# Attention stage: row sums taken on GpSimd and VectorE, reciprocals transposed on TensorE, and one timetable for a group of pixels

## The chip, the core and the metric

The kernel runs on one core of one Trainium2 chip. The metric is the device time of one execution in microseconds (us). A core has four compute engines that run side by side, each through its own instructions in order, and that wait for each other by semaphores: TensorE (PE in the profile, with its weight loads as PEld), VectorE (DVE), ScalarE (ACT) and GpSimd (POOL). SyncE (SP) issues the transfers. SBUF is the working memory; PSUM takes TensorE's results, and this kernel uses it in banks of 512 float32 columns.

## What is computed

The input x has 128 images of 128 channels and 32 x 32 pixels. Two layers follow each other; only the first, an attention layer, is touched by the change. Each of the 1024 pixels is a sequence of its own: the 128 images at that pixel attend to each other, with 4 heads of 32 channels.

```python
xs = x.reshape(B, C, L).transpose(2, 0, 1)                 # L=1024 pixels, B=128, C=128
q, k, v = jnp.split(xs @ in_proj_weight.T + in_proj_bias, 3, axis=-1)
q = q * float(hd) ** (-0.5)                                # 4 heads, hd = 32
scores = jnp.einsum('lhbd,lhed->lhbe', q, k)               # 128 x 128 per pixel and head
attn = jax.nn.softmax(scores, axis=-1)
out = jnp.einsum('lhbe,lhed->lhbd', attn, v)
y = out @ out_proj_weight.T + out_proj_bias + xs
y = (y - mu) * jax.lax.rsqrt(var + LN_EPS) * norm_weight + norm_bias
```

The second layer (convolutions and a selective scan, one image after the other) reads the first layer's result from the DRAM tensor `mid`.

## The kernel before

`attention_layer` works on groups of LG = 4 pixels, 256 groups in all. Channels lie on the partitions. SyncE brings 64 pixels of all images at a time into `xt` (two buffers), and results leave from `yt` (two buffers). All data are float32.

A group goes through these steps:

- GpSimd gathers its columns into `xg` (L221).
- TensorE projects q and k (L168, 512 columns each) and v (L233, per pixel). VectorE moves q out of PSUM with bias and scale (L209), ScalarE moves k (L226), VectorE moves v (L240).
- Scores (L142): per pixel and head one product of 32 rows, into the four PSUM banks of `s_ps`, one bank per head. A pixel's four heads use the four 32-row strips of the array at the same time.
- Softmax in two halves of two pixels: VectorE takes the maximum of each row (`top`, L152), VectorE subtracts it (`shifted`, L156) into `e`, ScalarE takes the exponential (`exps`, L165).
- Per pixel, TensorE transposes the four heads of `e` (L178); the result is copied to `eT`, by ScalarE for three pixels (L254, L256, L267) and by VectorE for one (L258).
- `weighted` (L183) multiplies twice per pixel: `eT` with v (the weighted sum, not yet divided) and `eT` with a matrix of ones 32 columns wide, so that each row sum comes out of TensorE and stands at once on all 32 channels of its head. Both use 32-column strips of the array, four heads at the same time.
- ScalarE forms the reciprocal of the sums as exp(-ln(sum)) into `rden` (L201, L202) and VectorE multiplies (L203, `oT`).
- Output projection with the mean over channels already taken off, and the residual, add up in one bank (L217, L218); ScalarE squares (L219), TensorE averages over channels (L228), ScalarE forms 1/sqrt as exp(-0.5 ln) (L229, L230), VectorE applies it (L242, `z`), GpSimd applies weight and bias into `yt` (L243).

The order on every engine is written out by hand in `tick`: one call issues the scores of one group, the transposes of the group before it, the end of the one before that, and so on, so that a period of all engines is one tick. Four PSUM banks (`m_ps`) are handed round in a fixed pattern. The constants of the second layer (`mamba_constants`, a generator) are prepared in pieces between the first ticks. Its first piece issues some thirty small weight loads on SyncE; here it stands behind the load of the first `xt`.

The second layer already uses another scheme: class `Plan` collects tasks with a name, an engine, the buffers that they read and write and the banks that they take and give. Each name has a due time in a table, tasks of image i are due i periods later, and `run` issues everything in order of due time. A due time only sets the order on each engine; nothing waits for a clock. `Plan` reads its table and period from the module's `AT` and `PERIOD`.

Of the kernel before, what the change touches and what calls it, by code (L numbers as in the profile page):

```python
# [50 lines left out]
@with_exitstack  # L51
def attention_layer(ctx: ExitStack, tc: tile.TileContext, ident, eps, x, w, mid, prepare):

    nc = tc.nc
    const = ctx.enter_context(tc.tile_pool(name="a_const", bufs=1))
    keep = ctx.enter_context(tc.tile_pool(name="a_keep", bufs=1))

    qkvT = const.tile([P, 3 * P], F32, name="qkvT")  # L60
    nc.sync.dma_start(qkvT, w["qkvT"])
    outT = const.tile([P, P], F32, name="outT")
    nc.sync.dma_start(outT, w["outT"])
    bqkv = const.tile([P, 3], F32, name="bqkv")
    nc.sync.dma_start(bqkv, w["qkv_b"])
    bo = const.tile([P, 1], F32, name="bo")
    nc.sync.dma_start(bo, column(w["out_b"]))
    nw = const.tile([P, 1], F32, name="nw")
    nc.sync.dma_start(nw, column(w["norm_w"]))
    nb = const.tile([P, 1], F32, name="nb")  # L70
    nc.sync.dma_start(nb, column(w["norm_b"]))
    qscale = float(HD) ** -0.5

    mean = const.tile([P, P], F32, name="a_mean")
    nc.vector.memset(mean, 1.0 / P)
    ones = const.tile([P, HD], F32, name="ones")
    nc.vector.memset(ones, 1.0)
    om = const.tile([P, 1], F32, name="om")  # L80
    nc.vector.reduce_sum(om, outT, AX.X)
    nc.vector.tensor_scalar_mul(om, om, 1.0 / P)
    outc = const.tile([P, P], F32, name="outc")
    nc.vector.tensor_scalar(outc, outT, om, None, ALU.subtract)
    resc = const.tile([P, P], F32, name="resc")
    nc.vector.tensor_sub(resc, ident, mean)
    by = const.tile([P, 1], F32, name="by")
    with tc.tile_pool(name="a_prep_ps", bufs=1, space=PSUM) as prep_ps:
        b_ps = prep_ps.tile([P, 1], F32, name="by_ps")
        nc.tensor.matmul(b_ps, lhsT=outc, rhs=bqkv[:, 2:3], start=True, stop=False)  # L90
        nc.tensor.matmul(b_ps, lhsT=resc, rhs=bo, start=False, stop=True)
        nc.vector.tensor_copy(by, b_ps)

    psum = ctx.enter_context(tc.tile_pool(name="a_psum", bufs=1, space=PSUM))
    xcol = x.rearrange("b c l -> c b l")
    ycol = mid.rearrange("b c l -> c b l")

    def several(n, shape, name, pool=keep):
        return [pool.tile(shape, F32, name=f"{name}{j}") for j in range(n)]

    GB = LG * NB
    PER = LB // LG
    xts = several(2, [P, NB, LB], "xt")
    xgs = several(4, [P, GB], "xg")
    yts = several(2, [P, NB, LB], "yt")
    qTs = several(2, [P, GB], "qT")
    kTs = several(2, [P, GB], "kT")
    vs = several(4, [P, LG, P], "v")
    es = several(2, [P, NH, LG, NB], "e")
    eTs = several(LG, [P, NH * NB], "eT")  # L110
    oT = keep.tile([P, GB], F32, name="oT")
    z = keep.tile([P, GB], F32, name="z")
    tops = several(2, [P, NH, LG // 2], "top")
    sq = keep.tile([P, GB], F32, name="sq")
    rden = keep.tile([P, GB], F32, name="rden")
    s_ps = psum.tile([P, NH, LG, NB], F32, name="s_ps")
    m_ps = several(4, [P, GB], "m_ps", psum)

    def load(l0, xt):
        for s in range(4):  # L120
            bs = slice(s * NB // 4, (s + 1) * NB // 4)
            nc.sync.dma_start(xt[:, bs, :], xcol[:, bs, ds(l0, LB)])

    def store(l0, yt):
        for s in range(4):
            bs = slice(s * NB // 4, (s + 1) * NB // 4)
            nc.sync.dma_start(ycol[:, bs, ds(l0, LB)], yt[:, bs, :])

    def pixels(ts, g):

        i = g % PER
        return ts[g // PER % 2][:, :, i * LG : (i + 1) * LG].rearrange("c b l -> c l b")

    def heads(h):
        return slice(h * HD, (h + 1) * HD)

    def scores(g, half):

        for i in range(half * LG // 2, (half + 1) * LG // 2):
            cs = slice(i * NB, (i + 1) * NB)  # L140
            for h in range(NH):
                nc.tensor.matmul(  # L142
                    s_ps[:, h, i, :],
                    lhsT=qTs[g % 2][heads(h), cs],
                    rhs=kTs[g % 2][heads(h), cs],
                    start=True,
                    stop=True,
                )

    def top(half):  # L150
        ls = slice(half * LG // 2, (half + 1) * LG // 2)
        nc.vector.tensor_reduce(tops[half], s_ps[:, :, ls, :], AX.X, ALU.max)  # L152

    def shifted(g, half):
        ls = slice(half * LG // 2, (half + 1) * LG // 2)
        nc.vector.tensor_tensor(  # L156
            es[g % 2][:, :, ls, :],
            s_ps[:, :, ls, :],
            tops[half].unsqueeze(3).to_broadcast([P, NH, LG // 2, NB]),
            ALU.subtract,  # L160
        )

    def exps(g, half):
        ls = slice(half * LG // 2, (half + 1) * LG // 2)
        nc.scalar.activation(es[g % 2][:, :, ls, :], es[g % 2][:, :, ls, :], AF.Exp)  # L165

    def project(g, j, bank):
        nc.tensor.matmul(  # L168
            bank,
            lhsT=qkvT[:, j * P : (j + 1) * P],  # L170
            rhs=xgs[g % 4],
            start=True,
            stop=True,
        )

    def transposed(g, i, bank):
        for h in range(NH):
            nc.tensor.transpose(bank[:, h * NB : (h + 1) * NB], es[g % 2][:, h, i, :], ident)  # L178

    def weighted(g, i, lhsT, bank):  # L180

        for h in range(NH):
            nc.tensor.matmul(  # L183
                bank[heads(h), i * NB : (i + 1) * NB],
                lhsT=lhsT(h),
                rhs=eTs[i][:, h * NB : (h + 1) * NB],
                start=True,
                stop=True,
            )

    def tick(t, p, a, s, c, d, y):

        pv, den, free, other = m_ps if t % 2 else (m_ps[3], *m_ps[1:3], m_ps[0])

        if s is not None:
            scores(s, 0)
            scores(s, 1)
        if d is not None:  # L200
            nc.scalar.activation(rden, den, AF.Ln)  # L201
            nc.scalar.activation(rden, rden, AF.Exp, scale=-1.0)  # L202
            nc.vector.tensor_mul(oT, pv, rden)  # L203
        if c is not None:
            exps(c, 0)
            exps(c, 1)
        if a is not None:
            project(a, 0, free)
            nc.vector.tensor_scalar(  # L209
                qTs[a % 2], free, bqkv[:, 0:1], qscale, ALU.add, ALU.mult  # L210
            )
        if s is not None:
            top(0)
            shifted(s, 0)
            top(1)
        if y is not None:
            nc.tensor.matmul(other, lhsT=resc, rhs=xgs[y % 4], start=True, stop=False)  # L217
            nc.tensor.matmul(other, lhsT=outc, rhs=oT, start=False, stop=True)  # L218
            nc.scalar.activation(sq, other, AF.Square, bias=by)  # L219
        if p is not None:  # L220
            nc.gpsimd.tensor_copy(  # L221
                xgs[p % 4].rearrange("c (l b) -> c l b", l=LG), pixels(xts, p)
            )
        if a is not None:
            project(a, 1, den)
            nc.scalar.activation(kTs[a % 2], den, AF.Identity, bias=bqkv[:, 1:2])  # L226
        if y is not None:
            nc.tensor.matmul(pv, lhsT=mean, rhs=sq, start=True, stop=True)  # L228
            nc.scalar.activation(sq, pv, AF.Ln, bias=eps)  # L229
            nc.scalar.activation(sq, sq, AF.Exp, scale=-0.5)  # L230
        if a is not None:
            for i in range(LG):
                nc.tensor.matmul(  # L233
                    free[:, i * P : (i + 1) * P],
                    lhsT=xgs[a % 4][:, i * NB : (i + 1) * NB],
                    rhs=qkvT[:, 2 * P : 3 * P],
                    start=True,
                    stop=True,
                )
            nc.vector.tensor_copy(vs[a % 4].rearrange("p l d -> p (l d)"), free)  # L240
        if y is not None:
            nc.vector.scalar_tensor_tensor(z, other, by, sq, ALU.add, ALU.mult)  # L242
            nc.gpsimd.tensor_scalar(  # L243
                pixels(yts, y),
# [1244 lines left out]
```

## Time and profile before

| What | us |
|---|---|
| Time, median of 3 runs | 15043.29 |
| lowest and highest of them | 15040.22 and 15054.52 |
| Profiled execution | 15073.08 |
| its span, first to last instruction | 15071.3 |
| first and last result of the attention stage (L243) | 60.93 and 2846.71 from the span's start |
| one tick of the attention stage (L243 at 1498.90 and at 1509.79) | 10.89 |

| Engine | busy us | share of the span |
|---|---|---|
| PE | 13455.7 | 89% |
| DVE | 13733.7 | 91% |
| ACT | 12058.3 | 80% |
| POOL | 12317.6 | 82% |

The span runs from the first instruction to the last; the small rest of the profiled execution lies around it. A profile line names the line of the kernel, the engine, the operation, output <- inputs, the shapes, a count and times. A float32 product is recorded as two passes, a transpose as one, so a 512-column product counts x2.

### The profile page before, as it was taken

What the parts mean: (1) busy time and instruction counts of PE and PEld (TensorE: products, weight loads), DVE (VectorE), ACT (ScalarE), POOL (GpSimd) and SP (SyncE); (2) the same over time, 40 slices, a digit from 0 to 9 for tenths busy, and PEclk for the clock granted to TensorE, in tenths of its full rate; (3) what the DMA queues carried; (4) which work ended last, traced back from release to release, by engine and by line L of the source; (5) the groups of instructions that cost most, each with busy time, mean ns of one, the idle gap of its engine ahead of it and who ended that gap; (6) DMA issues with size and microseconds to landing.
All of it is one profiled execution on the core that took longest, in us unless ns stands there. A gap on an engine that the chain in (4) does not pass through costs nothing. (4 is left out here: it accounts for less than half of the span.)

```text
span 15071.3 us, 229111 instructions
## 1 busy us (share of the span) xinstructions
PE 13455.7 (89%) x87094; PEld 6624.5 (44%) x87094; DVE 13733.7 (91%) x8754; ACT 12058.3 (80%) x19718; POOL 12317.6 (82%) x4361
## 2 busy tenths in 40 slices
PE   9999999888888888888888888888888888888887
PEld 6666666433333333333333333333333333333333
DVE  6777777599999999999999999999999999999999
ACT  5666666688888888888888888888888888888887
POOL 1222222299999999999999999999999999999999
PEclk9999999899999999999999999999999999999999
DMA  3222222266676666666666666666666666666665
GB/s 57 50 57 46 46 46 46 67 169 169 169 169 169 168 169 169 168 168 169 169 168 168 168 168 169 168 169 168 169 167 169 168 168 169 169 169 169 167 168 146
DMA packets 1191603, 2180.96 MB, mean 145 GB/s; under 512 B 673233, under 2 KB 674273, under 8 KB 1190497
## 3 DMA queue, kind: packets, MB, share of 16 engines
q1 hardware_dynamic: 1190496, 2166.31, 59.6%
q8 instruction: 682, 11.17, 0.3%
q14 instruction: 425, 3.47, 0.1%
HBM read 1746.30 MB, written 419.43 MB: 144 GB/s over the span
## 5 line engine op out<-in xcount | busy, mean ns | idle before, releaser
L1216 POOL TENSOR_TENSOR dbu<-dtxr,brep 128x2048 f32<-128x2048 f32 x1280 | 5805.4, 4552 | 27.7 <-DMA dtr<-dtd 13.3
L1262 POOL TENSOR_TENSOR hc<-hc,crep 128x1024 f32<-128x1024 f32 x2304 | 5412.3, 2372 | 310.5 <-PE da L1209 211.1
L1241 ACT ACTIVATE da<-dtr,aneg 128x1024 f32<-128x1024 f32 x2560 | 2956.6, 1163 | 510.3 <-DVE hc L1262 489.3
L1254 DVE TENSOR_TENSOR_SCAN hc<-da,dbu 128x1024 f32<-128x1024 f32 x1408 | 3162.1, 2276 | 103.6 <-ACT da L1241 94.9
L1155 ACT ACTIVATE bx<-p_ps,bT 128x128 f32<-128x128 f32 (+1 forms) x8192 | 2798.0, 486 | 132.1 <-PE p_ps L1147 131.9
L1254 DVE TENSOR_TENSOR_SCAN da<-da,dbu 128x1024 f32<-128x1024 f32 x1152 | 2622.7, 2287 | 115.3 <-ACT da L1241 106.9
L1209 PE MATMUL da<-ident,bx 128*128 128x128 f32 x12288 | 1828.7, 295 | 501.1 <-DVE hc L1254 417.6
L1209 PEld LDWEIGHTS da<-ident,bx 128*128 128x128 f32 x12288 | 1489.7, 150 | 1634.3 <-DVE hc L1254 1068.5
L1262 DVE TENSOR_TENSOR hc<-da,crep 128x1024 f32<-128x1024 f32 x1792 | 2162.8, 1219 | 47.8 <-PE y_ps L1281 6.5
L769 PE MATMUL p_ps<-tn,wk 128*128 128x512 f32 x4096 | 1989.5, 608 | 240.4 <-DVE tn L733 147.2
L1241 ACT ACTIVATE dbu<-dtr,aneg 128x1024 f32<-128x1024 f32 x1536 | 1734.3, 1218 | 473.2 <-DMA dtr<-dtd 471.1
L1254 DVE TENSOR_TENSOR_SCAN hc<-dbu,da 128x1024 f32<-128x1024 f32 x896 | 2000.1, 2268 | 24.3 <-ACT dbu L1241 21.4
L1281 PE MATMUL y_ps<-hc,fold 128*32 128x512 f32 x16384 | 1974.3, 599 | 37.6 <-POOL hc L1262 25.8
L1254 DVE TENSOR_TENSOR_SCAN da<-dbu,da 128x1024 f32<-128x1024 f32 x640 | 1451.1, 2282 | 196.4 <-PE da L1209 132.6
L221 POOL COPY xg<-xt 128x512 f32<-128x512 f32 x256 | 270.4, 1057 | 1223.2 <-PE m_ps L217 1199.3
L830 PE MATMUL p_ps<-xpad,dwd 64*64 64x512 f32 x9216 | 1153.4, 593 | 112.8 <-ACT xm L801 105.3
L769 PEld LDWEIGHTS p_ps<-tn,wk 128*128 128x128 f32 x4096 | 710.6, 191 | 1141.6 <-issue 776.3
L243 POOL TENSOR_SCALAR yt<-z,nw,nb 128x512 f32<-128x512 f32 x256 | 320.2, 1251 | 1032.7 <-DVE z L242 1032.7
L1281 PEld LDWEIGHTS y_ps<-hc,fold 128*32 128x32 f32 x16384 | 477.0, 109 | 1182.9 <-issue 858.3
L830 PEld LDWEIGHTS p_ps<-xpad,dwd 64*64 64x64 f32 x9216 | 362.4, 133 | 802.4 <-issue 568.4
L1025 POOL TENSOR_TENSOR dtt<-dtt,xm 128x1024 f32<-128x1024 f32 x256 | 608.5, 2377 | 120.9 <-DMA dtd<-dtt 109.8
L203 DVE TENSOR_TENSOR oT<-m_ps,rden 128x512 f32<-128x512 f32 x256 | 177.0, 691 | 566.2 <-ACT rden L202 566.2
(131 smaller groups left out, 19281.3 us busy)
## 6 DMA issues: line engine op xcount, KB each, us to landing
dtxr<-dtxd SPq DMA_DIRECT2D x2048, 256.0 KB, 5.5
dtr<-dtd SPq DMA_DIRECT2D x2048, 256.0 KB, 5.4
crep<-bcd SPq DMA_DIRECT2D x2048, 128.0 KB, 6.2
brep<-bcd SPq DMA_DIRECT2D x1536, 128.0 KB, 5.0
x<-mid SPq DMA_DIRECT2D x256, 512.0 KB, 5.9
dtd<-dtt SPq DMA_DIRECT2D x256, 512.0 KB, 5.2
dtxd<-dtt SPq DMA_DIRECT2D x256, 512.0 KB, 4.4
xt<-in_x SPq DMA_DIRECT2D x64, 1024.0 KB, 12.2
```

The source lines that it names most:

```text
L221: nc.gpsimd.tensor_copy(xgs[p % 4].rearrange("c (l b) -> c l b", l=LG), pixels(xts, p))
L243: nc.gpsimd.tensor_scalar(pixels(yts, y), z.rearrange("c (l b) -> c l b", l=LG), nw, nb, ALU.mult, ALU.add,)
L769: nc.tensor.matmul(a.tile, lhsT=wk[:, k, h * P : (h + 1) * P], rhs=tn[:, c * CH + k : (c + 1) * CH + k], start=k == 0, stop=c > 0 and k == ...
L830: nc.tensor.matmul(pair[r] .tile[c * HP : (c + 1) * HP] .rearrange("p (r q) -> p r q", q=HH), lhsT=dwd[rs, k, :], rhs=xpad[rs, y0 : y0 + r ...
L1025: lambda: nc.gpsimd.tensor_mul(dtt[h], dtt[h], im["xm"][h]),
L1155: nc.scalar.activation(bx[:, tb, ks, n, :], src, AF.Copy, scale=bT[:, j : j + 1])
L1209: nc.tensor.transpose(ps[:, tb * P : (tb + 1) * P], bx[:, tb, TENSOR[h, nb] * NDB + db].rearrange("p n d -> p (n d)"), ident,)
L1216: nc.gpsimd.tensor_mul(dbu[u // 2 % NDBU], dtxr[db // 2], brep[nb - 1].unsqueeze(1).to_broadcast([P, 2, L]),)
L1241: lambda: nc.scalar.activation(a, dtr[db // 2][:, db % 2, :], AF.Exp, scale=aneg[:, h * NDB + db, nb : nb + 1],),
L1254: lambda: nc.vector.tensor_tensor_scan(dst, a, b, 0.0, ALU.mult, ALU.add),
L1262: lambda: engine.tensor_mul(hc[u % 8], dst, crep[nb]),
L1281: nc.tensor.matmul(y_ps[db * GD : (db + 1) * GD, chunk(c)], lhsT=fold, rhs=hc[(i * NG + k) % 8][:, chunk(c)], start=False, stop=last,)
```

## The change

The attention stage is rewritten as tasks of a `Plan` with a table of its own; the second layer keeps its table and its tasks.

- `Plan` gets period and table as arguments. `A_PERIOD = 10.6` and `A_AT` are the attention stage's.
- Row sums: the products with ones are gone, and with them the matrix of ones. GpSimd adds the two halves of each row of `e` (128 to 64 numbers) and again (64 to 32), and VectorE sums the remaining 32 (`reduce_sum`).
- Reciprocals: VectorE's `reciprocal` reads the 8 sums of a half group, each repeated 32 times, and writes 256 numbers (`shared`). TensorE transposes `shared` for each of the four pixels (`spread`), ScalarE copies the result to `rden` (`shares`). The Ln and Exp of L201 and L202 are gone.
- v leaves PSUM by ScalarE instead of VectorE (`v_out`), and all four `eT` copies are ScalarE's (`EVICT` is empty).
- The two halves of a group are issued apart: on TensorE, scores, transposes and weighted products are interleaved pixel by pixel. `e` and `shared` have three buffers per half, `xg` five, v three, `sq` two; `z` is now written over `sq`.
- Banks are taken from a queue and given back in the order of the tasks.
- The first piece of `mamba_constants` is called ahead of the plan, so its loads are issued ahead of the first load of x. The other pieces are tasks (`part`) of groups 4 to 15.

By the table, one period in the steady state stands in this order. PE: v_mm, turned2, projected, turned1, q_mm, k_mm, variance, weighted0, scores0, weighted1, turned0, scores1, weighted2, turned3, weighted3, spread, residual. DVE: o_out, top0, shifted0, inverse1, q_out, shifted1, normed, inverse0, top1. ACT: kept2, v_out, squared, kept1, exps1, k_out, rstd, kept0, kept3, shares, exps0. POOL: picked, summed0, summed1, placed.

In the built program the first score product of a group waits for VectorE's `shifted1` of the group before, that is, for the second half too; the second half of the scores has no wait of its own. Behind the attention stage every engine has the same instructions in the same order as before.

```diff
-    def __init__(self, banks):
+    def __init__(self, banks, period, at):
+        self.period, self.times = period, at
...
-        t.at = t.image * PERIOD + AT[t.name]
+        t.at = t.image * self.period + self.times[t.name]
...
+NARROW = 32
+EVICT = ()
+PARTS = 12
+A_PERIOD = 10.6
+A_AT = {
+    "exps0": 31.49, "exps1": 35.83, "inverse0": 40.17, "inverse1": 45.93, "k_mm": 3.57,
+    "k_out": 5.09, "kept0": 39.28, "kept1": 45.83, "kept2": 43.94, "kept3": 40.89, "load": 0.01,
+    "normed": 60.62, "o_out": 53.09, "part": 16.29, "picked": 0.0, "placed": 61.67,
+    "projected": 54.12, "q_mm": 2.63, "q_out": 4.4, "residual": 51.64, "rstd": 58.87,
+    "scores0": 16.29, "scores1": 17.66, "shares": 52.09, "shifted0": 23.51, "shifted1": 26.32,
+    "spread": 51.07, "squared": 55.74, "store": 61.68, "summed0": 32.95, "summed1": 37.29,
+    "top0": 21.99, "top1": 19.84, "turned0": 38.29, "turned1": 44.46, "turned2": 42.95,
+    "turned3": 39.66, "v_mm": 31.38, "v_out": 33.94, "variance": 57.51, "weighted0": 47.85,
+    "weighted1": 48.65, "weighted2": 50.02, "weighted3": 50.83,
+}
...
-            nc.scalar.activation(rden, den, AF.Ln)
-            nc.scalar.activation(rden, rden, AF.Exp, scale=-1.0)
-            nc.vector.tensor_mul(oT, pv, rden)
...
-                weighted(c, i, lambda h: v[:, i, heads(h)], other)
-                weighted(c, i, lambda h: ones, den)
...
+            def summed():
+                src, w = e, NB // 2
+                while w >= NARROW:
+                    dst = halves[f][:, :, :, 0:w]
+                    nc.gpsimd.tensor_tensor(
+                        dst, src[:, :, :, 0:w], src[:, :, :, w : 2 * w], ALU.add
+                    )
+                    src, w = dst, w // 2
...
+            def inverse():
+                nc.vector.reduce_sum(sums[f], halves[f][:, :, :, 0:NARROW], AX.X)
+                nc.vector.reciprocal(
+                    share, sums[f].unsqueeze(3).to_broadcast([P, HL, NH, HD])
+                )
...
+        def spread():
+            for i in range(LG):
+                share = shared[i // HL][g % NE][:, i % HL]
+                nc.tensor.transpose(
+                    shares.tile[:, i * NB : (i + 1) * NB],
+                    share.rearrange("p h d -> p (h d)"),
+                    ident,
+                )
...
+            lambda: nc.scalar.copy(rden, shares.tile),
...
+            lambda: nc.vector.tensor_mul(oT, pv.tile, rden),
...
+    nc.scalar.preload_act_table_set("natural_log_exp_and_others")
+    next(parts)
+    with tc.manual_schedule():
+        plan.run()
```

## The prediction

> **What bounds the kernel now.** I read the page first, for where the attention stage lies:
>
> ```profile
> span 15071.3 us, 229111 instructions
> PE   9999999888888888888888888888888888888887
> POOL 1222222299999999999999999999999999999999
> ```
>
> GpSimd is nearly idle in the first eight of 40 slices: that is the attention stage, 0 to some 2850 us. Everything behind it is issued as before, so the change can move only this fifth of the span. Next the windows view, inside that stage (columns: time, PE, PEld, DVE, ACT, POOL busy, granted clock, DMA):
>
> ```profile
> 1000.00:2000.00 1000.00, 991.43 (x11946) 651.01 (x11936) 744.20 (x828) 685.97 (x1012) 211.51 (x184) 1.00 0.25 52
> ```
>
> TensorE is busy 99%, at full granted clock; VectorE 74%, ScalarE 69%, GpSimd 21%. A busy PE may still be waiting, so I read one tick of its timeline (start, duration of the group of passes, then line and tiles):
>
> ```profile
> 1501.55 1.17 PE L142 MATMUL s_ps<-kT,qT 32*128 32x128 f32 x32
> 1502.66 1.13 PE L168 MATMUL m_ps<-xg,qkvT 128*128 128x512 f32 x2
> 1503.62 1.02 PE L217 MATMUL m_ps<-xg,resc 128*128 128x512 f32 x2
> 1504.48 1.02 PE L218 MATMUL m_ps<-oT,outc 128*128 128x512 f32 x2
> 1505.34 1.02 PE L168 MATMUL m_ps<-xg,qkvT 128*128 128x512 f32 x2
> 1506.28 1.12 PE L228 MATMUL m_ps<-sq,a_mean 128*128 128x512 f32 x2
> 1507.24 1.05 PE L233 MATMUL m_ps<-qkvT,xg 128*128 128x128 f32 x8
> 1508.13 1.60 PE L178 MATMUL m_ps<-ident,e 128*128 128x128 f32 x12
> 1509.83 0.43 PE L183 MATMUL m_ps<-eT,v 128*32 128x128 f32 x8
> 1510.05 0.43 PE L183 MATMUL m_ps<-eT,ones 128*32 128x128 f32 x8
> 1510.40 0.66 PE L178 MATMUL m_ps<-ident,e 128*128 128x128 f32 x4
> 1510.99 0.43 PE L183 MATMUL m_ps<-eT,v 128*32 128x128 f32 x8
> ...
> 1512.11 0.40 PE L183 MATMUL m_ps<-eT,ones 128*32 128x128 f32 x8
> 1512.44 0.95 PE L142 MATMUL s_ps<-kT,qT 32*128 32x128 f32 x24
> ```
>
> Starts, not durations, tell the cost. A 512-column product takes 0.86 us (1503.62 to 1504.48), v 0.89, a transpose 0.11, eight narrow passes 0.22 (1509.83 to 1510.05), the scores' 32 passes 0.89 where they run freely. Changing the array's shape costs too. Four transposes between narrow products take 0.59 for 0.44, and two narrow blocks before a transpose 0.57 (1509.83 to 1510.40) for 0.44: a turn between wide and narrow is some 0.14. From the last narrow block (1512.11 + 0.22) over the scores to the second product behind them (1503.62), 0.43 is spent beside the passes: 0.21 for each turn of the scores. Passes per tick: five 512-column products 4.30, v 0.89, 16 transposes 1.75, 64 narrow passes 1.76, scores 0.89, sum 9.59; turns 3 x 0.14 + 0.43 = 0.85; the remaining 0.44 of 10.88 is waiting, for `squared` before L228, and for VectorE's `v` copy and `z` around the transposes. PE's order bounds the stage.
>
> **The change, part by part.** These rows (groups view and page; busy, mean ns, idle) price what moves:
>
> ```profile
> L202 ACT ACTIVATE rden<-rden 128x512 f32<-128x512 f32 x92 | 58.1, 632 | 2.9
> L201 ACT ACTIVATE rden<-m_ps 128x512 f32<-128x512 f32 x92 | 55.1, 598 | 81.8 <-PE m_ps L183 81.8
> L152 DVE TENSOR_REDUCE top<-s_ps 128x8 f32<-128x1024 f32 x184 | 223.5, 1215 | 0.0
> L1262 POOL TENSOR_TENSOR hc<-hc,crep 128x1024 f32<-128x1024 f32 x2304 | 5412.3, 2372 | 310.5 <-PE da L1209 211.1
> ```
>
> *ScalarE:* 7.69 per tick by its rows, less 598 + 632 ns, plus three 0.59 copies (v, third eT, shares): 8.23. *GpSimd:* by 2372 ns for 1024 and 4552 for 2048 (the dbu rows), 2.13 ns per number and 0.19: 1.28 and 0.74 per half, so 1.06 + 1.25 + 4.04 = 6.35. Both stay under 10.6, beside TensorE. *VectorE:* 8.44 per tick by its rows (two L152, two L156 at 1220 ns, 751 for q, 744 for z, three at 692), less the copies of v and one eT, 2 x 0.69. The reduce of 256 numbers, between 288 ns for 128 (om) and 1215 for 1024, is 0.42. No reciprocal is in this trace. From below it is bounded by the 256-number scaling of inzT (348 ns), from above by the only reciprocal there is, Ln and Exp, 1.23 us; the scan, VectorE's slowest row with 2276 ns for 1024, would give 0.7. I take 0.42, one number per cycle like the reduce, its neighbour in shape and engine. VectorE is then 8.44 - 1.38 + 4 x 0.42 = 8.74.
>
> [...]
>
> GpSimd's new work runs beside VectorE. VectorE's 1024-wide operations on PSUM take 1220 ns here with GpSimd 21% busy (L156) and 1219 ns in the second stage (L1262) with GpSimd 97% busy, so I charge nothing for it. [...]
>
> *TensorE alone:* ones removed 4 x 0.22, spread added 4 x 0.11: passes 9.59 - 0.88 + 0.44 = 9.15. But by the new order there are nine turns where there were five: five wide/narrow (0.70), into the scores from narrow and from wide (0.42), and twice from scores to narrow, which the trace does not show: 0.14 to 0.21, I take 0.16 since it is the narrow weights that are loaded. That is 1.44, and 10.59 if nothing waits.
>
> *The new wait:* scores0 of a group waits for `shifted1` of the group before. That closes a loop. Counted from one scores0 to the next: TensorE issues scores0, weighted1, turned0, scores1, weighted2, turned3, weighted3, spread with their turns (0.45 + 0.16 + 0.22 + 0.14 + 0.44 + 0.21 + 0.45 + 0.16 + 0.22 + 0.14 + 0.44 + 0.14 + 0.22 + 0.14 + 0.44, and 0.17 until the result stands) 4.14; ScalarE's `shares` 0.59 and 0.05 of handing over; then VectorE, in its order, o_out 0.69, top0 1.22, shifted0 1.22, reduce 0.42, reciprocal 0.42, q_out 0.75, shifted1 1.22, less 0.08 at the four seams where the next start overlaps, plus 0.25 for handing over and late weights: 5.87. Sum 10.65. Behind the waiting scores stand weighted1, turned0 and all the rest of TensorE, so the loop is the period when it exceeds 10.59. normed, inverse0 and top1 (0.75 + 0.84 + 1.22 = 2.81) stand outside it, in the 4.78 us in which the loop is with TensorE and ScalarE: 2.0 us of cover, and once that is gone a dearer inverse0 counts as well. I take 10.65: 10.885 - 10.65 = 0.235, times 256 is 60 us saved.
>
> *The ends:* two SP lines of the timeline give the price of the moved first piece:
>
> ```profile
> 17.85 4.68 SPq L445 DMA_DIRECT2D w1T<-in_cv1T  x1
> 33.43 16.15 SPq L122 DMA_DIRECT2D xt<-in_x  x4
> ```
>
> Those loads hold SP from 17.85 to 33.43; now they stand ahead of the first x, and everything waits for that: 15.6 us lost, with nothing to hide it (the first gather starts at 25.21 behind x). A group now passes through six periods instead of four, which costs in the fill and comes back in the drain, where the last group has the engines to itself: 0, give or take 10. The `part` tasks cost 11 us of longer ticks before (12.17, 16.68 and 15.05) and the same after.
>
> Sum: -60 + 15.6 = -45 us. The profiled execution's 15073.1 would become 15028; it stands 30 above the median of the runs, 15043.3, so that becomes 14998. About 0.2% (30 us) is what a measurement of this kernel can tell from no change.
>
> **The rivals.** *Turns eat the gain* (0.20): if scores to narrow costs 0.21 or more, or the other turns lose 0.03 each, the loop and TensorE reach 10.8 to 10.95: 15035 to 15075. For it: four more turns, the most of any part; against: the five old ones cost 0.85 together, which leaves little room for dearer ones.
>
> *The reciprocal is dear* (0.22), the case on the other side. Place: inverse1, inside the loop, each ns a ns of period. The change breaks even at a reciprocal of 0.60 us (0.42 + 0.235 - 0.06 of start), and is slower by over 0.2% from 0.72. At 1.23 us the period is 11.46: 256 x 0.575 + 15.6 = 163 us more, 15206. For it: the kernel before makes its reciprocals on ScalarE though VectorE had 2.4 us free per tick; against: every plain VectorE row takes about 1 ns per number.
>
> *The wait falls away* (0.03): turns overlap, and the period is 10.4: -124 + 16, 14935.
>
> **How the numbers follow.** My forecast (0.55) spans periods of 10.5 to 10.75: 14960 to 15025; a tenth of it lies within 0.2%. Faster: 0.50 + 0.03; same: 0.05 + 0.13 of the turns; slower: 0.07 of the turns and 0.22. Own range 14960 to 15025; to hold eight in ten it must reach over the turns into the dear reciprocal, up to its bound: 14955 to 15206, which leaves out about 0.15 above and 0.03 below.
>
> **What would show it.** L543's period in steady state near 10.65, its first start 20 to 30 us later than 60.93; TensorE still 98% busy; RECIPROCAL rows near 420 ns and, at scores0, short waits on `shifted`. A reciprocal over 0.7 us, or VectorE above 90% busy with TensorE waiting for `shifted`, would prove me wrong; so would a turn from scores to narrow above 0.3.

## The result, and the profile after

The changed kernel takes 15309.02 us (median of 4 runs, 15292.56 to 15315.25), the kernel before 15047.81 (15040.22 to 15054.52) beside it: a ratio of 1.0174, with a 95% interval of 1.0161 to 1.0186. The forecast was 14998, at most 15206. The change is slower, and by more than the rival that was priced for this side.

The profiled execution took 15292.56 us, the lowest of its four. Its last result of the attention stage (L543) starts at 3094.2 us; before it was 2846.71. So the stage is 247.5 us longer. Behind it, where nothing was changed, this execution is 28 us shorter than the profiled one before (12196.5 against 12224.6); in the profiled runs below, with the same instructions there, that part takes between 12215 and 12224, so this is no effect of the change. The other three runs of the changed kernel take 14 to 23 us more than the profiled one.

The page, where the forecast began:

```profile
DVE  7999999969999999999999999999999999999999
```

VectorE now reads 9 in nearly all slices of the attention stage, where it read 7 in the kernel before:

```profile
DVE  6777777599999999999999999999999999999999
```

The windows view inside the stage (time, PE, PEld, DVE, ACT, POOL busy, granted clock, DMA):

```profile
1000.00:2000.00 1000.00, 905.18 (x8640) 547.31 (x8639) 903.32 (x933) 652.31 (x1016) 531.96 (x509) 1.00 0.25 47
```

TensorE fell from 991 to 905 busy of 1000, VectorE rose from 744 to 903. The clock is still 1.00. The costliest groups on the page (busy, mean ns, idle) tell what VectorE and GpSimd do:

```profile
L382 POOL TENSOR_TENSOR halved<-e 128x512 f32<-128x512 f32 x512 | 650.7, 1271 | 365.8 <-ACT e L405 365.0
L412 DVE RECIPROCAL shared<-total 128x256 f32<-128x256 f32 x512 | 897.6, 1753 | 17.8
```

GpSimd's additions take 1.27 and 0.73 (1.28 and 0.74 were taken) and the reduce 0.41 (0.42 taken), as forecast. The reciprocal takes 1753 ns; 420 were taken, and 1230 was the upper bound. The timeline shows where it stands, from one scores0 (L365) to the next, here with some of the lines between them:

```profile
1500.94 0.73 PE L365 MATMUL s_ps<-kT,qT 32*128 32x128 f32 x16 [0.70 <-DVE e L374]
...
1505.19 0.58 ACT L489 COPY rden<-m_ps 128x512 f32<-128x512 f32 x1
...
1505.81 0.69 DVE L497 TENSOR_TENSOR oT<-m_ps,rden 128x512 f32<-128x512 f32 x1 [1.05 <-ACT rden L489]
...
1508.81 0.41 DVE L411 TENSOR_REDUCE total<-halved 128x8 f32<-128x256 f32 x1
...
1509.25 1.75 DVE L412 RECIPROCAL shared<-total 128x256 f32<-128x256 f32 x1
...
1510.92 0.65 DVE L323 TENSOR_SCALAR qT<-m_ps,bqkv 128x512 f32<-128x512 f32 x1
...
1511.49 1.22 DVE L374 TENSOR_TENSOR e<-s_ps,top 128x1024 f32<-128x1024 f32 x1
...
1512.76 0.73 PE L365 MATMUL s_ps<-kT,qT 32*128 32x128 f32 x16 [0.70 <-DVE e L374]
```

This is the loop of the prediction, link by link: TensorE 4.25 (1500.94 to 1505.19), ScalarE's `shares` with its handing over 0.62, VectorE's seven steps 6.95 (o_out at 1505.81, top0, shifted0, reduce, reciprocal, q_out, shifted1, to the scores at 1512.76), sum 11.82. TensorE waits 0.70 at scores0 for `shifted1` of the group before, and VectorE waits 1.05 for `rden` at o_out: both wait once per period, which is how a loop through several engines looks when none of them is full. In the waits view of 1000 to 2000 us (total us, times, longest) these two are VectorE's only wait and the larger of TensorE's two; the other, 34.9 us, is weighted0's for q_out (L323), the step right ahead of `shifted1`:

```profile
DVE oT L497 <- ACT rden L489: 87.9, 84, 1.0
...
PE s_ps L365 <- DVE e L374: 59.9, 85, 0.7
```

### The profile page after: what moved, and what is told of

It reads as the page before. It is cut to its first block, busy times and chain, and to the rows that moved or that the text cites. A ratio compares the mean times of both kernels' runs of the same rounds, so it can differ in the third digit from the quotient of the medians.

```text
span 15290.7 us, 216576 instructions
## 1 busy us (share of the span) xinstructions
PE 13415.5 (88%) x79926; PEld 6465.6 (42%) x79926; DVE 14387.9 (94%) x9265; ACT 12102.6 (79%) x19974; POOL 13331.2 (87%) x5385
## 5 line engine op out<-in xcount | busy, mean ns | idle before, releaser
L437 ACT COPY eT<-m_ps 128x512 f32<-128x512 f32 x1024 | 602.1, 588 | 1009.5 <-PE m_ps L429 650.8
L382 POOL TENSOR_TENSOR halved<-e 128x512 f32<-128x512 f32 x512 | 650.7, 1271 | 365.8 <-ACT e L405 365.0
L412 DVE RECIPROCAL shared<-total 128x256 f32<-128x256 f32 x512 | 897.6, 1753 | 17.8
```

Of the source, the lines that this page charges most:

```text
L382: nc.gpsimd.tensor_tensor(dst, src[:, :, :, 0:w], src[:, :, :, w : 2 * w], ALU.add)
L412: nc.vector.reciprocal(share, sums[f].unsqueeze(3).to_broadcast([P, HL, NH, HD]))
```

## The experiments

Each ratio compares a run with the kernel before on the same chip. The periods are median distances of L543's starts, or of the same instruction where its line has another number.

### 1. A copy in place of the reciprocal

```diff
-                nc.vector.reciprocal(
+                nc.vector.tensor_copy(
                     share, sums[f].unsqueeze(3).to_broadcast([P, HL, NH, HD])
                 )
```

> The changed kernel, with VectorE's reciprocal of 256 numbers replaced by a copy of the same 256 numbers from the same repeated input (the division is left out). If the reciprocal's duration is the one term of the sum that failed, the copy takes about 0.42 us, the period falls from 11.82 to 10.65 and the time to about 14998 us (14975 to 15025). If the turns between array shapes, GpSimd's additions or the new order cost more than the sum says, the period stays at 10.8 or more: 15035 us or above.

Measured: 15003.44 us against 15063.38, ratio 0.9959 (0.9947 to 0.9972), that is 60 us less than the kernel before. The period is 10.56, and TensorE is busy all the time again:

```profile
1000.00:2000.00 1000.00, 1000.00 (x9645) 612.85 (x9641) 841.20 (x1044) 730.14 (x1137) 597.15 (x568) 1.00 0.27 52
```

So nearly everything lost lies in that one instruction; the rest of the sum held to 0.1 us a period. In the loop the copy takes 0.29 us, 0.13 less than the 0.42 of the sum: the loop would be 10.52, less than TensorE's own 10.59, and the period is TensorE's. The other copy, outside the loop, took much longer. Timeline of both, each with the GpSimd instruction nearest to it:

```profile
1501.86 0.73 POOL L382 TENSOR_TENSOR halved<-halved 128x256 f32<-128x256 f32 x1
...
1502.62 0.29 DVE L412 COPY shared<-total 128x256 f32<-128x256 f32 x1
...
1506.86 1.24 POOL L543 TENSOR_SCALAR yt<-sq,nw,nb 128x512 f32<-128x512 f32 x1 [0.86 <-DVE sq L536]
...
1507.12 1.13 DVE L412 COPY shared<-total 128x256 f32<-128x256 f32 x1
```

The first copy starts when GpSimd has just become free (1502.59). The second starts while GpSimd works until 1508.10, and ends at 1508.25. That holds for all 254 copies that were issued while L543 ran: each ended 0.144 to 0.150 us behind the end of the GpSimd instruction. Experiment 6 follows that up.

### 2. The reciprocal of the 8 sums alone

```diff
+                nc.vector.reciprocal(sums[f], sums[f])
-                nc.vector.reciprocal(
+                nc.vector.tensor_copy(
                     share, sums[f].unsqueeze(3).to_broadcast([P, HL, NH, HD])
                 )
```

> The changed kernel, with the reciprocal taken of the 8 sums alone (in place) and spread over 256 numbers by a copy on VectorE. If the reciprocal costs about 6.4 ns for each number and 0.12 us once, it takes some 0.17 us here; the copy stands where the prediction had its reciprocal of 0.42, so the loop gets 0.15 us longer than 10.65: period 10.8, time about 15035 us (15010 to 15060). If the reciprocal has a large cost of its own whatever the count, each inverse stays near 2 us and the period is 12 or more: above 15340 us.

Measured: 15031.09 us, ratio 0.9979 (0.9971 to 0.9988); the reciprocal takes 203 ns, the period is 10.69:

```profile
1500.14 0.20 DVE L412 RECIPROCAL total<-total 128x8 f32<-128x8 f32 x1
```

The cost goes with the count (203 ns for 8 numbers, 1753 for 256), and the loop prices it: reduce, reciprocal and copy in the loop are 0.41 + 0.20 + 0.29 = 0.90, where the sum had 0.84, so 10.65 + 0.06 = 10.71. The change with this one repair is 0.2% faster than the kernel before.

### 3. inverse1 moved out of the loop

```diff
-    "exps0": 31.49, "exps1": 35.83, "inverse0": 40.17, "inverse1": 45.93, "k_mm": 3.57,
+    "exps0": 31.49, "exps1": 35.83, "inverse0": 40.17, "inverse1": 47.6, "k_mm": 3.57,
```

> The changed kernel with one number of the timetable altered: inverse1 is due at 47.6 and not 45.93, so that VectorE does it right behind shifted1 instead of ahead of q_out and shifted1. The reciprocal keeps its 1.75 us. If the loop (scores0 waits for shifted1 of the group before) sets the period, 2.1 us of inverse1 leave it, VectorE's own sum (10.67 us busy per period and some waiting) becomes the bound, and the period falls from 11.82 to about 11.1: 256 x 0.7 = 180 us less, about 15125 us (15090 to 15190). If VectorE's load alone sets the period already, it stays within 0.1 of 11.82: 15280 to 15335 us.

Measured: 15088.11 us, ratio 1.0016 (1.0007 to 1.0025), 37 us below the expected 15125 and just below its range. One number of the table is worth some 240 us (the ratio falls from 1.0174 to 1.0016), with every duration unchanged. The period is 10.87, and VectorE is now the bound:

```profile
1000.00:2000.00 1000.00, 996.25 (x9386) 598.12 (x9385) 978.69 (x1013) 723.18 (x1106) 580.54 (x552) 1.00 0.25 48
```

VectorE works 10.64 of 10.87 us (978.69 by 92.0 periods). VectorE has no wait in the waits view of these 1000 us. The loop theory holds; its rival, that VectorE's load alone gave 11.82, is out. The expected 11.1 had left VectorE more waiting than it has.

### 4. What the reciprocal costs by size

```diff
+    def measured():
+        probe = sqs[0]
+        nc.vector.memset(probe, 2.0)
+        eight = probe[:, 0:8].unsqueeze(2).to_broadcast([P, 8, HD])
...
+        for _ in range(4):
+            nc.vector.reciprocal(to[0][:, 0:8], probe[:, 0:8])
...
+            nc.vector.reciprocal(to[0][:, 0:512], probe)
+            nc.vector.reciprocal(eights(to[0]), eight)
+            nc.vector.tensor_copy(eights(to[0]), eight)
+            nc.scalar.copy(eights(to[1]), eight)
+            nc.gpsimd.tensor_copy(eights(to[2]), eight)
...
     with tc.manual_schedule():
+        measured()
         plan.run()
```

> The changed kernel with a block of extra VectorE work ahead of the first group, four times over: reciprocals of 8, 64, 128, 256 and 512 numbers that lie side by side, one of 8 numbers each read 32 times, a copy of 8 numbers each read 32 times, and that same copy on ScalarE and on GpSimd. If the reciprocal itself is slow, the 256 side by side and the 8 x 32 both take about 1.75 us, 512 some 3.4 and 8 some 0.17 (6.4 ns for each number and 0.12). If reading one number 32 times is what is slow, 256 side by side take about 0.42 us and the copy of 8 x 32 about 1.75. ScalarE's copy about 0.40, GpSimd's 0.3 to 0.75 us. The block delays the start by some 30 us, so the whole time is about 15340 us and tells nothing else.

Measured, in the groups view of the first 80 us (the last column is idle time before):

```profile
L568 DVE RECIPROCAL e<-sq 128x512 f32<-128x512 f32 x4 | 13.4, 3353 | 0.1
...
L567 DVE RECIPROCAL e<-sq 128x256 f32<-128x256 f32 x4 | 7.0, 1749 | 0.1
L569 DVE RECIPROCAL e<-sq 128x256 f32<-128x256 f32 x4 | 6.8, 1708 | 0.0
...
L570 DVE COPY e<-sq 128x256 f32<-128x256 f32 x4 | 1.2, 295 | 0.1
...
L564 DVE RECIPROCAL e<-sq 128x8 f32<-128x8 f32 x4 | 0.8, 197 | 0.0
```

256 numbers side by side (L567) cost about the same as 8 numbers read 32 times each (L569), 1749 and 1708 ns: it is the operation, not the repeated read. The step from 256 to 512 numbers costs 1604 ns, so 6.27 ns per number, which leaves 0.15 us once; 64 took 553 and 128 took 953 ns. The copy of the same 8 x 32 takes 295 ns. ScalarE's copy took 403 ns and GpSimd's 402. The whole time, 15311.95 us in one run, did not rise as expected: the block (1.75 to 37.40 us) stands in time in which the first group waits for x anyway (first gather in after at 37.5).

### 5. The first load of x ahead of the constants again

```diff
-            add("load", "SP", lambda b=b: load(b))
+            if b:
+                add("load", "SP", lambda b=b: load(b))
...
+    load(0)
     next(parts)
```

> The changed kernel with the first load of x issued ahead of the first piece of mamba_constants again, as before the change; nothing else differs. If the some thirty loads ahead of x cost the start what the trace of after shows (first gather at 37.48, before at 25.21), the first gather starts near 25, the last result of the stage comes some 12 us earlier than 3094.2, and the time is about 15297 us (15280 to 15310). If the first loads are held by something else (the weight loads of the attention layer that stand ahead of both), the first gather stays above 33.

Measured: the first gather starts at 25.0 (after: 37.5), the first result at 70.3 (82.0), the last of the stage at 3085.5 (3094.2), 8.7 us earlier, where 12 were expected. One tick with a constants' part grew from 11.94 to 13.38, and one near the end of the stage from 11.19 to 12.70; these take back 3 us of the 11.7 by which the first result came earlier. The second stands in experiment 4's run as well (12.69), which loads x as the changed kernel does, so it isn't this edit's. The whole time, 15310.12 us in one run where about 15297 was expected, can't show so little. SyncE's lines of the timeline tell the size of the term; after first, then this run:

```profile
3.54 0.43 SPq L588 DMA_DIRECT2D w1T<-in_cv1T  x1
...
14.88 34.18 SPq L278 DMA_DIRECT2D xt<-in_x  x8
```

```profile
17.45 4.76 SPq L590 DMA_DIRECT2D w1T<-in_cv1T  x1
```

Behind x (3.54 to 17.45), the first constant's issue alone holds SyncE for 4.76 us; ahead of x it takes 0.43, and the whole piece is done in 11.3 us (3.54 to 14.88).

### 6. Two inputs in place of the copy

```diff
-                nc.vector.reciprocal(
-                    share, sums[f].unsqueeze(3).to_broadcast([P, HL, NH, HD])
-                )
+                total = sums[f].unsqueeze(3).to_broadcast([P, HL, NH, HD])
+                nc.vector.tensor_tensor(share, total, total, ALU.max)
```

> As the run with the copy in place of the reciprocal, but the 256 numbers are written as the maximum of the repeated sums with themselves (two inputs; the division is left out). In the run with the copy, one copy took 0.29 us while GpSimd stood idle and 1.13 us where a GpSimd instruction ran beside it, and it ended just behind that instruction. If that wait belongs to the fast one-input copy, the two-input form takes one number per cycle, 0.41 to 0.44 us every time, period 10.55 to 10.65 and time near 15003 us (14985 to 15025). If any VectorE work on SBUF has to wait for GpSimd, its durations spread from 0.3 to over 1.1 us as well.

Measured: 14995.42 us, ratio 0.9961 (0.9947 to 0.9974), period 10.58. The time is as expected, the durations are not. One period, the instruction inside the loop first:

```profile
1503.71 0.42 DVE L413 TENSOR_TENSOR shared<-total 128x256 f32<-128x256 f32 x1
...
1507.95 1.23 POOL L542 TENSOR_SCALAR yt<-sq,nw,nb 128x512 f32<-128x512 f32 x1 [0.86 <-DVE sq L535]
1508.20 1.08 DVE L413 TENSOR_TENSOR shared<-total 128x256 f32<-128x256 f32 x1
```

Alone it takes 0.42 (at 1503.71); beside L542 it too ends only when GpSimd has ended (1509.18, and 1509.28). So it is not the one-input copy alone that waits. But not all VectorE work on SBUF waits: a GpSimd instruction runs during 510 of the 512 reduces L411 of this run, and all take 401 to 411 ns; in the trace of after the reciprocal takes 1752 to 1755 whatever GpSimd does. What waited here is the copy (0.29 us alone) and the form with two SBUF inputs (0.42 alone). Both end just behind GpSimd's instruction: 0.10 us here, 0.144 to 0.150 in experiment 1. Why these two wait and the reduce and the reciprocal do not, no run here shows.

### 7 and 8. The repaired change with fewer turns

Both take the reciprocal of the 8 sums, spread it with a copy that is a task of its own, load x first, and use another timetable. In 7 the copy is GpSimd's, in 8 VectorE's. The diff of 8, with its table:

```diff
+                nc.vector.reciprocal(sums[f], sums[f])
-                nc.vector.reciprocal(
-                    share, sums[f].unsqueeze(3).to_broadcast([P, HL, NH, HD])
-                )
-            add(f"inverse{f}", "DVE", inverse, reads=[f"half{f}"], writes=[kt])
+            add(f"inverse{f}", "DVE", inverse, reads=[f"half{f}"], writes=[f"total{f}"])
+            add(
+                f"cast{f}",
+                "DVE",
+                lambda: nc.vector.tensor_copy(
+                    share, sums[f].unsqueeze(3).to_broadcast([P, HL, NH, HD])
+                ),
+                reads=[f"total{f}"],
+                writes=[kt],
+            )
...
+    "cast0": 32.856, "cast1": 26.767, "exps0": 26.791, "exps1": 21.58, "inverse0": 31.929,
+    "inverse1": 26.191, "k_mm": 8.772, "k_out": 9.52, "kept0": 31.866, "kept1": 31.616,
+    "kept2": 29.835, "kept3": 35.554, "load": 0.01, "normed": 48.952, "o_out": 40.444,
+    "part": 8.773, "picked": 0.0, "placed": 53.698, "projected": 43.296, "q_mm": 9.54,
+    "q_out": 11.676, "residual": 42.384, "rstd": 47.991, "scores0": 17.763, "scores1": 16.598,
+    "shares": 39.012, "shifted0": 25.635, "shifted1": 21.102, "spread": 36.43, "squared": 43.625,
+    "store": 53.703, "summed0": 30.327, "summed1": 22.881, "top0": 22.206, "top1": 18.893,
+    "turned0": 31.473, "turned1": 30.531, "turned2": 28.433, "turned3": 35.265, "v_mm": 13.924,
+    "v_out": 14.133, "variance": 46.712, "weighted0": 36.45, "weighted1": 36.661,
+    "weighted2": 36.961, "weighted3": 37.411,
```

> Reciprocal of the 8 sums alone on VectorE (0.20 us), spread over 256 numbers by a copy on GpSimd (0.40 us), the first load of x ahead of the constants, and another timetable for the group: TensorE's order is q_mm, turned3, variance, weighted0 to weighted3, scores0, scores1, spread, v_mm, turned2, residual, k_mm, turned0, projected, turned1, so that the array changes its shape three times per period and not nine. By the prediction's own terms: passes 9.15, turns 0.14 + 0.21 + 0.21 = 0.56, period 9.71 if nothing waits; 256 x 1.17 = 300 us less than before: about 14755 us (14700 to 14850). If the turns cost little and a wait that the sum does not know sets the period, it stays at 10.4 or more: 14930 us or above.

> The same idea with the copy of 256 numbers on VectorE and a timetable of its own (weighted0 to weighted3 together, scores0 and scores1 together, three turns per period too). If the copy only waits where a GpSimd instruction runs beside it (0.3 to 1.3 us), VectorE still has room (some 8.5 of 9.7) and the period is 9.7 to 10.0: 14755 to 14835 us. If that wait stands on the way to scores0 each time, the period is above 10.1: 14860 us or more.

Measured: 7 takes 14770.36 us, ratio 0.9812 (0.9799 to 0.9826), 8 takes 14760.67, ratio 0.9804 (0.9791 to 0.9818); the kernel before took 15053.76 beside them. Both times lie in the expected ranges. The periods are 9.66 and 9.64, here as means behind the first twelve distances, since single ones run from 8.07 to 11.26; 9.71 was expected for 7, and 9.7 to 10.0 for 8. In 7, TensorE's lines where the array changes its shape:

```profile
1508.34 1.08 PE L449 MATMUL m_ps<-eT,v 128*32 128x128 f32 x32
1509.35 1.17 PE L366 MATMUL s_ps<-kT,qT 32*128 32x128 f32 x32
1510.45 0.66 PE L481 MATMUL m_ps<-ident,shared 128*128 128x128 f32 x4
```

By starts: into the narrow products 0.96 for 0.86 (the product L536 starts at 1507.38), from there into the scores 1.01 for 0.88, out of them 1.10 for 0.89: 0.10 + 0.13 + 0.21 = 0.44 for three turns, 0.56 expected. With 9.15 of passes that is 9.59 of 9.66. So the prediction's prices carry to another order: the passes as they are, the turns 0.12 too dear in sum. In 8, the windows view shows TensorE full and VectorE with room, and 500 of the 512 copies (L419) took 0.28 to 0.30 us: they start where GpSimd is idle, though in 264 of them a GpSimd addition starts before they end. The other 12 start while a GpSimd instruction runs and take 0.64 to 1.21:

```profile
1000.00:2000.00 1000.00, 1000.00 (x10547) 686.32 (x10549) 852.09 (x1350) 805.13 (x1244) 647.47 (x622) 1.00 0.29 56
```

The 10 us between 7 and 8 are 13.6 us at the end of the stage in the profiled executions (2557.7 and 2544.1): 8 from the start (the thirteenth result at 219.1 and 210.9), the rest from the period. How much of the gain over experiment 2 is the timetable's and how much the load's was not run apart; by experiment 5 the load is at most 12 us of it.

## Why the prediction was wrong

**The step that failed: the reciprocal's price.** The term was 0.42, taken after the reduce. It measured 1.753 us, 1.33 more, and stood inside the loop. The taken value was the author's estimate from the kind of neighbour, not from the operation: the reduce's two rows (288 ns for 128 numbers, 1215 for 1024) give 1.03 ns per number, while the reciprocal's sizes in experiment 4 give 6.27. No run shows the "cycle" that the prediction counts by. The bounds were rows of other work: 0.348 is a scaling, and 1.23 is ScalarE's Ln and Exp of 512 numbers. Neither is a bound on an operation that the trace does not show: a different way to a reciprocal, on another engine, says nothing about how dear this one can be. So the range ended at 15206, and the result lies above it.

**With the right price the rest of the sum gives the period to 0.16 us.** The loop, 10.65 + 1.33 = 11.98, measured 11.82. Its links: TensorE 4.25 (4.14 in the sum), ScalarE 0.62 (0.64), VectorE 6.95 (5.87 + 1.33 = 7.20). VectorE's 0.25 less is mainly q_out, 0.65 and not 0.75, and a handing over of 0.05 and not 0.25 at scores0; TensorE's 0.11 more takes some of it back. Times 256, the 1.17 between 10.65 and 11.82 is 299 us. The stage ended 292 us later than forecast (3094 against 2847 - 60 + 15.6 = 2802): those 299, less 3 at the start, and 4 that are not assigned.

**The loop** (scores0 waits for shifted1) was right: link by link in the timeline, and by experiment 3, where 0.95 us of the period went by moving one task.

**TensorE alone, 10.59:** right to 0.03. With the reciprocal out of the way (experiment 1) the period was 10.56 with TensorE always busy. The turn from scores to narrow, taken as 0.16, is 0.21 (in after, 1500.94 to 1501.60 for 0.45 of passes), so the condition of the rival "Turns eat the gain" was met, but not its price: the turns into the scores are 0.14 and 0.15 by the starts of experiment 1, where 0.21 each was taken, and so the errors nearly cancel.

**The start, 15.6:** the sign was right, 12.3 measured. The constants were priced where they stand behind x, with 4.68 us for the first issue; ahead of x that issue takes 0.43.

**GpSimd beside VectorE, nothing charged:** right for this change, whose reduce (404 to 411 ns in the trace of after) and reciprocal (1752 to 1755) take the same beside GpSimd's work. It does not hold for the copy of experiment 1, 0.29 us alone and 1.13 beside L543, or for the two-input form of experiment 6, 0.42 and 1.08.

**The rivals:** "The reciprocal is dear" (0.22) is what happened: at inverse1, inside the loop, each ns a ns of period, slower from 0.72 us; only its price of 1.23 us was too low. Both signs that the prediction named against itself came: a reciprocal over 0.7 us, and VectorE 90% busy with TensorE waiting for `shifted`. Experiment 6, whose instruction takes just the 0.42 of the sum inside the loop, shows what the forecast was worth had the price held: a period of 10.58 against 10.65, and a ratio of 0.9961 (0.9947 to 0.9974), where 14998 to 15043.3 is 0.9970.

## What to carry to other kernels

An operation that no row shows has no upper bound from its neighbours (here 1.23 us by them, 1.753 measured): look at what it does for each number, and do it on as few numbers as possible before spreading the result (8 instead of 256 numbers here: 203 ns instead of 1753). Write down the loops that an order closes, with every task in them; a dear task is cheap once it stands outside, and moving one task by a line of the order was worth some 240 us. On TensorE, the count of changes of the array's shape belongs in the sum: with nine per group down to three, each 0.09 to 0.21 us by the starts in experiments 1 and 7, the same passes went from 10.56 us (experiment 1) to 9.66 (7).

## What the hardware showed

- VectorE's reciprocal: 0.15 us and 6.27 ns per number, about the same for numbers side by side and for repeated reads (1749 and 1708 ns for 256, experiment 4); 256 numbers took 1752 to 1755 ns in all 512 reciprocals of the changed kernel, 510 of them beside a GpSimd instruction.
- A one-input copy from SBUF to SBUF of 256 float32 numbers takes 0.29 us; if GpSimd's L543 is under way when it is issued, it ends 0.144 to 0.150 us behind that instruction's end (254 of 254 in experiment 1). A two-input form takes 0.42 us and waits in the same way, to 0.09 to 0.11 us behind (254 of 254 in experiment 6); the reduce of 256 numbers does not: it takes 401 to 411 ns there, a GpSimd instruction running during 510 of 512. Where such copies stand beside GpSimd's work is thus part of their price: 0.29 or 1.13 us in experiment 1.
